# Newton's roots on VectorE for the gathered sums of a mixture-of-experts decoder, with two smaller moves

## The chip, the cores and the metric

The kernel runs on one core of a Trainium2 chip. A core has five engines with a queue of instructions each: TensorE (PE in the profile, with its weight loads as PEld), VectorE (DVE), ScalarE (ACT), GpSimd (POOL) and SyncE (SP), which issues most of the plain transfers. Indirect transfers, the gathers and scatters by an index, are issued by GpSimd. The metric is the device time of one execution in microseconds (us).

## The reference, cut to what matters

Four decoder layers work on 8 sequences of 256 tokens with 256 features. Each layer has a self-attention, a cross-attention and a feed-forward part; after each part the result is added to its input and normalised:

```python
def _layernorm(x, axis=-1, eps=1e-05):
    m = jnp.mean(x, axis=axis, keepdims=True)
    v = jnp.var(x, axis=axis, keepdims=True)
    return (x - m) / jnp.sqrt(v + eps)

x = _layernorm(x + _L0_attn_ref(x, ...))
x = _layernorm(x + _L0_xattn_ref(x, ctx_1024, ...))
x = _layernorm(x + _L0_ffn_ref(x, ...))
...                      # the same for L1, L2 and L3
```

The feed-forward parts of L0, L1 and L2 are mixtures of experts: a router scores the experts, every token takes its two best, and the two experts' outputs are added with weights. L1's has 8 experts with a limited capacity, so the place (rank) of a token in its expert's list matters:

```python
probs = jax.nn.softmax(xn @ router_w.T, axis=-1)
topk_p, topk_i = jax.lax.top_k(probs, K)          # K = 2
order = jnp.argsort(~sel, axis=1, stable=True)
dispatch = order[:, :capacity]
```

L3's first part is a state-space layer that begins with an RMS norm of x without a mean, `x * rsqrt(mean(x*x) + eps) * w`, and has no router anywhere.

## The kernel before

**Tiles.** The 2,048 tokens are 16 tiles of 128 tokens by 256 features (`NT`), two tiles to a sequence; a pair of tiles is a batch b (`NB` = 8), and four tiles are a block (`NBLK` = 4). The tiles of x stay on the chip from one part to the next. All of it is one program without loops at run time: Python generators write the instructions, and a scheduler decides the order of each engine's queue from the order in which they are written and from what depends on what. Pieces of one stage are put between those of another by hand: `self.later` appends a generator, and each `self.tick` takes one piece (up to the next `yield`) of the oldest one.

**Layer norm.** `norm` (L245) takes the mean and variance of a tile with `bn_stats` (L249) and `bn_aggr` (L251) on VectorE, then calls `rsqrt` (L179): two GpSimd instructions, the addition of eps (L182) and a power of −0.5 (L183). VectorE then subtracts the mean and multiplies by the root (L255). All layer norms of the kernel go through it.

**Routing.** `Routing.batch` (from L2484) routes one pair during the cross-attention, in pieces. The first piece is the scores, the softmax, the two best experts (`rhot`, `rsel` at L2535) and the running counts (`rbefore`, L2538). The next piece multiplies by a triangle and by ones on TensorE to count each token's rank (the helper `mm`, L155), works out the place in the expert's list (L2547 to L2560), and scatters the tile's rows there (L1018, GpSimd). In the kernel before, one empty piece stands between the two in L2 alone (`if kind == 2: yield`, L2540). In L0's and L1's cross-attention, `cross64`, the ticks stand in `outputs` between the products of the weights with V (L947), the transposes of the weights (L932) and the copies of these (L141 on VectorE, L143 on ScalarE).

**Gathered sums.** The next layer's attention takes the experts' outputs back: `Routing.collected().sums(b)` gathers two rows for each token of a pair (`gather`, L1055, into gy), adds them with their weights on VectorE (L2680), and calls `norm`. Two gy buffers for each of the two choices hold four gathers at most under way. In L0 to L1 and L1 to L2 the tiles are then transposed (`put_xT`, L235). An order is forced between one add and the next (`g.gate`).

**L3's first part.** From L2 to L3, `norm` also leaves the mean square of the normalised tile, v/(v+eps), in `ms` (L260). `block` (L1990) takes a root of four of these by `rsqrt` (`r4`), scales four tiles of x by it on GpSimd (`xb`, L1999) and transposes them on TensorE (L293) to `xr`. The products of the block follow (`steps`), and among them the step sizes dt by a chain of small VectorE instructions (L2014 to L2027) that ends in `ad`. In the first block, pieces of L3's keys (`l3_keys`, with a softmax whose last step is GpSimd's L2246) stand between. For each pair, `weights` makes decays (L2128 on ScalarE, L2130 on VectorE, exponentials L2140, products L2154), and `outputs` the gate (`zs`, L2180), the sum of squares on TensorE (`onec`) and the residual (L2196).

**Newton's roots.** `roots` (L1609) exists in the kernel before and is used for L2's and L3's wide statistics of 16 and 32 columns. It takes a first guess of 1/sqrt(v) from the bits of v by a shift and a subtraction, and improves it three times:

```python
        nc.vector.tensor_scalar(v, v, scale, eps, ALU.mult, ALU.add)
        nc.vector.tensor_single_scalar(u.bitcast(I32), v.bitcast(I32), 1, op=ALU.logical_shift_right)
        nc.vector.tensor_scalar(y.bitcast(I32), u.bitcast(I32), -1.0, float(0x5F3759DF), ALU.mult, ALU.add)
        for _ in range(3):
            nc.vector.tensor_tensor(u, y, y, ALU.mult)
            nc.vector.scalar_tensor_tensor(u, u, -0.5, v, ALU.mult, ALU.mult)
            nc.vector.scalar_tensor_tensor(y, u, 1.5, y, ALU.add, ALU.mult)
```

That is 12 VectorE instructions, each on the result of the one before. The buffer of u (`hu`) is single, that of y (`hy`) double.

Of the kernel before, what the change touches and what calls it, by code (L numbers as in the profile page):

```python
# [14 lines left out]
AF = mybir.ActivationFunctionType  # L15
ALU = mybir.AluOpType
# [4 lines left out]
P = 128  # L21
NB = 8
S = 256
D = 256
# [5 lines left out]
LN_EPS = 1e-5  # L30
# [31 lines left out]
class Build:  # L62
# [179 lines left out]
        self.norm(i, r)  # L242
        self.put_xT(i, self.X[i])

    def norm(self, i, r, square=False):  # L245

        nc = self.nc
        st = self.t(self.sm, [P, 6], "st")
        nc.vector.bn_stats(st, r)  # L249
        mv = self.t(self.sm, [P, 2], "mv")  # L250
        nc.vector.bn_aggr(mv, st)  # L251
        rs = self.t(self.sm, [P, 1], "rs")
        self.rsqrt(rs, mv[:, 1:2], 1.0, LN_EPS)
        t = self.t(self.xp, [P, D], "x", bufs=20)
        nc.vector.tensor_scalar(t, r, mv[:, 0:1], rs, ALU.subtract, ALU.mult)  # L255
        self.X[i] = t
        if square:
            if i % 4 == 0:
                self.ms[i // 4] = self.t(self.sm, [P, 4], "ms", bufs=2)
            nc.vector.scalar_tensor_tensor(  # L260
                self.ms[i // 4][:, i % 4 : i % 4 + 1], mv[:, 1:2], rs, rs, ALU.mult, ALU.mult
            )

    def add_row(self, i, row):

# [1340 lines left out]
        nc.vector.tensor_scalar(m, m, 1.0 / 16, None, ALU.mult)  # L1606
        nc.vector.tensor_tensor(v, v, m.unsqueeze(2).to_broadcast([rows, n, 16]), ALU.subtract)

    def roots(self, v, scale, eps):  # L1609

        nc = self.nc
        rows, n = v.shape
        y, u = (self.t(self.sm, [P, 32], name, bufs=k)[:rows, :n] for name, k in (("hy", 2), ("hu", 1)))
        nc.vector.tensor_scalar(v, v, scale, eps, ALU.mult, ALU.add)
        nc.vector.tensor_single_scalar(u.bitcast(I32), v.bitcast(I32), 1, op=ALU.logical_shift_right)  # L1615
        nc.vector.tensor_scalar(y.bitcast(I32), u.bitcast(I32), -1.0, float(0x5F3759DF), ALU.mult, ALU.add)
        for _ in range(3):
# [3 lines that stand above are left out]
        return y  # L1621
# [304 lines left out]
    def l3_attn(self):  # L1926
        nc, a = self.nc, self.a
        with ExitStack() as ctx:
# [61 lines left out]
            def block(blk):  # L1990

                self.need(2 * blk)
                out = xrs[blk] = self.t(w2, [P, 2, 512], "xr")
                r = self.t(self.sm, [P, 4], "r4")
                self.rsqrt(r, self.ms[blk], 1.0, 1e-5)
                yield
                for t in range(4):
                    x = self.t(self.tmp, [P, D], "xb")
                    nc.gpsimd.tensor_scalar(x, self.X[4 * blk + t], r[:, t : t + 1], 1.0, ALU.mult, ALU.mult)  # L1999
                    self.transpose_to(out[:, :, t * P : (t + 1) * P], x, 2)  # L2000
                yield
                yield from steps(blk, out)

            def steps(blk, xr):
# [36 lines left out]
                sts[blk] = dt, cs, csT.rearrange("p i s -> p (i s)")  # L2041

            front = block(0)
            for _ in range(2):
                next(front)
# [168 lines left out]
            for b in range(NB):  # L2214
                blk = b // 2
                if b % 2 == 0 and blk + 1 < NBLK:
                    following = block(blk + 1)
                    next(following)

                self.tick()  # L2220
                E, xd = weights(b, cv, *sts[blk])
                last = (b, cv, zs, E, xd)
                if b + 1 < NB:
                    if b % 2:
                        for _ in following:
                            pass
                    cv, zs = inputs(b + 1, xrs[(b + 1) // 2])
                    next(following, None)
                self.settle(1)
                self.later(outputs(*last))  # L2230
# [218 lines left out]
class Routing:  # L2449
# [34 lines left out]
    def batch(self, b):  # L2484
        g, nc, E, kind = self.g, self.g.nc, self.E, self.kind
        two = slice(2 * b, 2 * b + 2)
        f = lambda name, sh, dt=F32: g.t(g.keep, sh, name, dt, bufs=2)
        if kind:
            r = self.r[:, two]
# [5 lines left out]
        if kind == 2:  # L2495
            for t in range(2):
                x = g.t(g.keep, [P, D], "rx", bufs=2)
# [6 lines left out]
        m = f("rm", [P, 2])  # L2504
# [31 lines left out]
        for t in range(2):  # L2536
            i = 2 * b + t
            g.routed = nc.vector.tensor_tensor(self.before[:, i + 1, :], self.before[:, i, :], sel[:, t, :], ALU.add)  # L2538
        yield
        if kind == 2:  # L2540
            yield

        ps = g.ps()[:, : 2 * E].rearrange("p (t e) -> p t e", t=2)
# [126 lines left out]
    def collected(self):  # L2670


        g, nc = self.g, self.g.nc

        def sums(b):
            for i in (2 * b, 2 * b + 1):
                for k in range(2):
                    y = g.t(g.keep, [P, D], f"gy{k}", bufs=2)
                    g.gather(y, self.eo, self.src[:, k, i : i + 1])
                    add = nc.vector.scalar_tensor_tensor(g.X[i], y, self.wt[:, k, i : i + 1], g.X[i], ALU.mult, ALU.add)  # L2680
                    if g.gate is not None:
                        g.after(add.ins, [g.gate.ins])
                    if g.gates:
                        g.after(add.ins, [g.gates.pop().ins])
                    g.gate = add
                g.norm(i, g.X[i], self.kind == 2)

        sums(0)
        yield
        for b in range(NB):  # L2690
            if self.kind != 2:
                for i in (2 * b, 2 * b + 1):
                    g.put_xT(i, g.X[i])
            if b + 1 < NB:
                sums(b + 1)
            yield
# [194 lines left out]
```

## Time and profile before

The median of three runs is 3623.32 us (3618.66 to 3629.59). The profiled execution is another one: 3594.94 us, with a span of 3593.2 us and a mean granted TensorE clock of 0.896. All times inside the kernel are those of this execution, counted from the start of its span.

| stretch, us | what | TensorE busy | VectorE busy | ScalarE busy | GpSimd busy |
|---|---|---|---|---|---|
| 1069–1140 | L0's sums, start of L1's attention | 44.0 of 71 | 39.6 | 11.4 | 43.5 |
| 1140–1440 | rest of L1's attention | 278.6 of 300 | 165.9 | 89.9 | 34.0 |
| 1440–1712 | L1's cross-attention with routing | 246.9 of 272 | 188.1 | 85.9 | 74.6 |
| 2245–2318 | L1's sums, start of L2's attention | 59.4 of 73 | 39.6 | 19.0 | 42.6 |
| 2318–2560 | rest of L2's attention | 207.3 of 242 | 157.4 | 97.2 | 44.1 |
| 2994–3133 | L2's sums, L3's first block, keys | 100.8 of 139 | 75.3 | 30.4 | 71.1 |
| 3133–3370 | rest of L3's first part | 188.6 of 237 | 179.8 | 101.8 | 52.0 |

A line of the timeline gives start, duration, engine, source line, operation, output and inputs, shapes, and in brackets how long the engine stood idle before it and what released it. A line of the groups gives busy time, mean ns of one, and the idle time before. A wait is named "who waits <- for whom: us in total, times, longest".

### The profile page before, as it was taken

How to read it: one execution, taken by the hardware profiler on the slowest of the kernel's cores; microseconds unless marked ns; L12 is line 12 of the kernel's file. 1: busy time of each engine (PE TensorE's matmuls, PEld its weight loads, DVE VectorE, ACT ScalarE, POOL GpSimd, SP SyncE). 2: the span in 40 equal slices, each digit the busy share in tenths (PEclk: the TensorE clock that was granted, in tenths of full speed). 3: DMA queues.
4: the chain of work that ended last, by engine and by line, in shares of the span. 5: the costliest groups of instructions: out<-in, count | busy, mean ns of one | idle time of the engine just before them, and what ended most of it. 6: DMA issues, size and time to landing. Idle time of an engine off the chain costs nothing. (4 is left out here: it accounts for less than half of the span.)

```text
span 3593.2 us, 49384 instructions
## 1 busy us (share of the span) xinstructions
PE 3102.3 (86%) x19146; PEld 2184.7 (61%) x19146; DVE 1834.9 (51%) x4823; ACT 1043.6 (29%) x2343; POOL 928.1 (26%) x1398
## 2 busy tenths in 40 slices
PE   4777589979997998998999999898787997778789
PEld 3444257658875665666555777565555785566556
DVE  7888546631116555776211221566675344677652
ACT  4666322212222332332111111344222111343311
POOL 2222513243314101222000000411343444312351
PEclk6777689979998999988999999999777998888889
DMA  9900100035541000001010333200002552000000
GB/s 338 305 2 1 48 7 19 19 108 181 179 144 47 1 25 25 13 14 60 15 36 0 119 124 119 62 1 8 7 19 83 198 196 77 22 1 7 12 5 19
DMA packets 132127, 239.47 MB, mean 67 GB/s; under 512 B 14568, under 2 KB 103920, under 8 KB 124208
## 3 DMA queue, kind: packets, MB, share of 16 engines
q1 hardware_dynamic: 107632, 136.25, 11.3%
q0 software_dynamic: 23104, 98.95, 7.9%
q8 instruction: 154, 2.52, 0.3%
q10 hardware_dynamic: 1152, 1.05, 0.1%
q14 instruction: 85, 0.70, 0.1%
HBM read 156.52 MB, written 79.69 MB: 66 GB/s over the span
## 5 line engine op out<-in xcount | busy, mean ns | idle before, releaser
L155 PE MATMUL ps<-xt,w 128*128 128x256 f32 (+1 forms) x1408 | 452.9, 472 | 3.3 <-issue 2.9
L155 PE MATMUL ps<-w,hT 128*128 128x256 f32 (+1 forms) x1792 | 397.4, 379 | 0.0
L155 PEld LDWEIGHTS ps<-w,hT 128*128 128x128 f32 (+1 forms) x1792 | 329.9, 186 | 56.5 <-issue 6.0
L155 PE MATMUL ps<-gT,w 128*128 128x256 f32 (+1 forms) x1472 | 357.4, 401 | 5.7 <-ACT gT L143 3.0
L155 PEld LDWEIGHTS ps<-xt,w 128*128 128x128 f32 x1408 | 268.7, 198 | 149.4 <-issue 125.0
L155 PEld LDWEIGHTS ps<-gT,w 128*128 128x128 f32 x1472 | 276.5, 191 | 76.8 <-ACT gT L143 3.9
L155 PE MATMUL ps<-w,oT 128*128 128x256 f32 x768 | 181.9, 390 | 3.3 <-DVE mv L251 1.8
L267 POOL TENSOR_TENSOR xb<-x,rows 128x256 f32<-128x256 f32 x96 | 71.6, 752 | 401.7 <-DVE res L272 393.7
L155 PEld LDWEIGHTS ps<-w,oT 128*128 128x128 f32 x768 | 146.4, 194 | 38.5 <-issue 14.1
L235 PE MATMUL ps<-ident,x 128*128 128x128 f32 x320 | 62.0, 307 | 79.5 <-DVE x L255 59.4
L1115 ACT ACTIVATE hT<-ps,more 128x256 f32<-128x256 f32 x152 | 71.9, 474 | 196.1 <-PE ps L155 196.1
L255 DVE TENSOR_SCALAR x<-res,mv,rs 128x256 f32<-128x256 f32 x128 | 57.4, 449 | 126.9 <-POOL rs L183 126.9
L1126 DVE COPY y<-ps 128x512 f32<-128x512 f32 x41 | 28.3, 690 | 174.7 <-PE ps L155 174.7
L1184 DVE TENSOR_TENSOR hT<-hT,ps 128x512 f32<-128x512 f32 x56 | 38.5, 688 | 154.2 <-PE ps L155 152.7
L677 ACT ACTIVATE e<-ps,nm 128x128 bf16<-128x128 f32 (+1 forms) x256 | 103.9, 458 | 40.1 <-DVE nm L672 24.1
L932 PE MATMUL ps<-ident,P 128*77 128x128 f32 x512 | 90.0, 303 | 25.5 <-POOL P L923 15.7
L1666 POOL TENSOR_TENSOR kpad<-kpad,rows 128x256 f32<-128x256 f32 (+1 forms) x10 | 7.3, 729 | 404.2 <-DVE hu L1615 316.9
L923 POOL TENSOR_TENSOR P<-P,z 128x1232 f32<-128x1232 f32 x24 | 54.1, 2252 | 219.6 <-DVE z L921 214.3
L183 POOL TENSOR_TENSOR rs<-rs,mhalf 128x1 f32<-128x1 f32 x192 | 106.1, 554 | 14.2
L932 PEld LDWEIGHTS ps<-ident,P 128*77 128x77 f32 x512 | 60.7, 157 | 73.4 <-issue 25.5
L947 PE MATMUL ps<-PT,V 77*64 77x256 f32 x512 | 98.5, 446 | 7.5 <-DVE PT L141 4.9
L1180 ACT ACTIVATE hT<-ps 128x512 f32<-128x512 f32 x56 | 33.4, 597 | 237.5 <-PE ps L155 237.5
(655 smaller groups left out, 6319.2 us busy)
## 6 DMA issues: line engine op xcount, KB each, us to landing
l2x<-zero SPq DMA_DIRECT2D x28, 1024.0 KB, 11.3
l0x<-zero SPq DMA_DIRECT2D x16, 1024.0 KB, 11.3
w<-in_L_ffn_rg SPq DMA_DIRECT2D x8, 1024.0 KB, 7.0
w<-in_L_ffn_ru SPq DMA_DIRECT2D x8, 1024.0 KB, 5.0
w<-in_L_ffn_rd SPq DMA_DIRECT2D x8, 1024.0 KB, 5.7
l2e<-y SPq DMA_DIRECT2D x22, 256.0 KB, 2.3
rows<-in_rows SPq DMA_DIRECT2D x9, 544.0 KB, 3.7
l0e<-y SPq DMA_DIRECT2D x19, 256.0 KB, 2.9
```

The costliest lines, as they stand in the source:

```text
L155: self.nc.tensor.matmul(out, lhsT, rhs, start=(i == 0), stop=(i == last))
L183: self.nc.gpsimd.tensor_tensor(out, out, self.mhalf[: in_.shape[0], :w], ALU.pow)
L235: self.nc.tensor.transpose(ps[:, k * P : (k + 1) * P], x[:, k * P : (k + 1) * P], self.ident)
L255: nc.vector.tensor_scalar(t, r, mv[:, 0:1], rs, ALU.subtract, ALU.mult)
L267: self.nc.gpsimd.tensor_tensor(t, self.X[i], row, ALU.add)
L677: nc.scalar.activation(e[:, : (t + 1) * P], ps[j][:, i, :], AF.Exp, bias=nm[:, t, h : h + 1], accum_out=z[:, t, h : h + 1],)
L923: eng.tensor_tensor(pr, pr, z.unsqueeze(2).to_broadcast([P, H, SC]), ALU.mult)
L932: nc.tensor.transpose(psv[:, m, t * P : (t + 1) * P], Pt[t][:, 2 * n + m, :], self.ident)
L947: nc.tensor.matmul(po[64 * m : 64 * m + 64, :S], V[:, h * 64 : (h + 1) * 64], ahead[n % 2][:, m, :], start=True, stop=True,)
L1115: nc.scalar.activation(hT[:, f + m, :], ps[:, m * 256 : (m + 1) * 256], func, bias=more[:, f + m : f + m + 1])
L1180: nc.scalar.activation(hT[:, f, :], ps, func, **({"bias": bias(f)} if bias else {}))
L1184: nc.vector.tensor_tensor(hT[:, f, :], hT[:, f, :], ps, ALU.mult)
```

## The change

There are three edits.

- **Gathered sums.** `sums(b)` no longer calls `norm`. It takes the statistics of both tiles of the pair, then one `roots` on the two variances (128x2), then the two normalises. From L2 to L3, the mean squares of the pair come from two 128x2 multiplications. The layer norms outside the gathered sums keep `norm` and its GpSimd root. `norm` loses its argument `square`.
- **Rank products.** In `batch`, the empty piece between the counts and the rank products stands in L1 as well as in L2.
- **L3's scaled x.** `block` takes `r4` by `roots` on VectorE, and the four scalings of x are ScalarE activations (Copy with a scale per token). `roots` gets an argument `src`, so that it can read another tile than it writes.

```diff
-    def norm(self, i, r, square=False):
+    def norm(self, i, r):
...
-        if square:
-            if i % 4 == 0:
-                self.ms[i // 4] = self.t(self.sm, [P, 4], "ms", bufs=2)
-            nc.vector.scalar_tensor_tensor(
-                self.ms[i // 4][:, i % 4 : i % 4 + 1], mv[:, 1:2], rs, rs, ALU.mult, ALU.mult
-            )
...
-    def roots(self, v, scale, eps):
+    def roots(self, v, scale, eps, src=None):
...
-        nc.vector.tensor_scalar(v, v, scale, eps, ALU.mult, ALU.add)
+        nc.vector.tensor_scalar(v, v if src is None else src, scale, eps, ALU.mult, ALU.add)
...
-                r = self.t(self.sm, [P, 4], "r4")
-                self.rsqrt(r, self.ms[blk], 1.0, 1e-5)
+                r = self.roots(self.t(self.sm, [P, 4], "r4"), 1.0, 1e-5, self.ms[blk])
                 yield
                 for t in range(4):
                     x = self.t(self.tmp, [P, D], "xb")
-                    nc.gpsimd.tensor_scalar(x, self.X[4 * blk + t], r[:, t : t + 1], 1.0, ALU.mult, ALU.mult)
+                    nc.scalar.activation(x, self.X[4 * blk + t], AF.Copy, scale=r[:, t : t + 1])
...
         yield
-        if kind == 2:
+        if kind:
             yield
...
         def sums(b):
+            mv = g.t(g.sm, [P, 2, 2], "mv2", bufs=2)
             for i in (2 * b, 2 * b + 1):
...
-                g.norm(i, g.X[i], self.kind == 2)
+                st = g.t(g.sm, [P, 6], "st")
+                nc.vector.bn_stats(st, g.X[i])
+                nc.vector.bn_aggr(mv[:, i - 2 * b, :], st)
+            rs = g.roots(g.t(g.sm, [P, 2], "v2", bufs=2), 1.0, LN_EPS, mv[:, :, 1])
+            for i in (2 * b, 2 * b + 1):
+                t = g.t(g.xp, [P, D], "x", bufs=20)
+                k = i - 2 * b
+                nc.vector.tensor_scalar(t, g.X[i], mv[:, k, 0:1], rs[:, k : k + 1], ALU.subtract, ALU.mult)
+                g.X[i] = t
+            if self.kind == 2:
+
+                if b % 2 == 0:
+                    g.ms[b // 2] = g.t(g.sm, [P, 4], "ms", bufs=2)
+                m = g.ms[b // 2][:, 2 * (b % 2) : 2 * (b % 2) + 2]
+                nc.vector.tensor_tensor(m, rs, rs, ALU.mult)
+                nc.vector.tensor_tensor(m, m, mv[:, :, 1], ALU.mult)
```

## The prediction

> **What bounds the kernel now.** I read the busy shares first.
>
> ```profile
> PE 3102.3 (86%) x19146; PEld 2184.7 (61%) x19146; DVE 1834.9 (51%) x4823; ACT 1043.6 (29%) x2343; POOL 928.1 (26%) x1398
> ```
>
> TensorE is busy for 86% of the span. Only the other 491 us can be won, and only where the change touches what ends a TensorE wait. The view of waits names the ones concerned (total, times, longest):
>
> ```profile
> DVE x L255 <- POOL rs L183: 200.9, 176, 4.8
> POOL rs L182 <- DVE mv L251: 174.0, 100, 16.4
> PEld L155 <- DVE rsel L2535: 40.8, 17, 3.7
> ```
>
> The 200.9 us are VectorE's, mostly in layernorms that the change leaves alone. The groups by form split off the gathered sums: 48 normalises, with 58.8 us of idle time put down to the root.
>
> ```profile
> L255 DVE TENSOR_SCALAR x<-x,mv,rs 128x256 f32<-128x256 f32 x48 | 23.8, 496 | 59.5 <-POOL rs L183 58.8 <-POOL kv L2262 0.3
> ```
>
> Then the timeline, for what TensorE itself waits on. GpSimd between L0 and L1:
>
> ```profile
> 1112.80 0.96 POOL L1055 DMA_INDIRECT gy<-l0e,rsrc  x1 [0.30 <-issue]
> 1113.83 0.19 POOL L182 TENSOR_SCALAR rs<-mv 128x1 f32<-128x1 f32 x1
> 1114.29 0.97 POOL L1055 DMA_INDIRECT gy<-l0e,rsrc  x1 [0.27 <-issue]
> 1115.29 0.58 POOL L183 TENSOR_TENSOR rs<-rs,mhalf 128x1 f32<-128x1 f32 x1
> ```
>
> Roots and gather issues share one queue. A gather takes 1.25 us of it alone and the two root instructions of a tile about 1.0 us. The TensorE waits, one line from each place:
>
> ```profile
> 1135.34 0.59 PE L1278 MATMUL ps<-later,identb 128*128 128x512 bf16 x1 [11.91 <-DVE kT L1251]
> 2290.50 1.01 PE L1522 MATMUL ps<-ones,onesb 128*128 128x512 bf16 x2 [4.92 <-DVE w L1455]
> 3026.82 1.61 PE L293 MATMUL ps<-ident,xb 128*128 128x128 f32 x6 [5.11 <-POOL xb L1999]
> 3060.11 1.01 PE L155 MATMUL ps<-kv 77*128 77x128 f32 x4 [14.13 <-DVE w L2276]
> 1493.26 0.18 PE L155 MATMUL ps<-rsel,upper 128*128 128x8 bf16 x1 [1.15 <-DVE rsel L2535]
> 3300.47 0.81 PE L155 MATMUL ps<-ad,triu 128*128 128x8 f32 x3 [5.45 <-DVE ad L2027]
> ```
>
> **What the Trainium skill says.** "PSUM — Partial Sum Buffer", Engine vs sequencer instructions: the queues of ScalarE, VectorE and GpSimd are strictly first in, first out. The trace agrees: kT L1251 starts at 1134.60, just behind an add that waited for its gather until 1134.20. "VectorE: DVE Perf Modes", Rules for kernel authors: for chained operations the count matters; the trace has 0.17 to 0.19 us for each small L1614–L1620 instruction. "SBUF — State Buffer", two separate sides: VectorE and GpSimd lock a shared port pair against each other. Rarely seen here: one L1616 of 1.12 us against its usual 0.17. "ScalarE: Activation LUTs", What ACT_TABLE_LOAD costs: about 1.28 us and as much again of drain; the trace has the 1.28, and the next activation starts at once.
>
> **The change, part by part.** The instruction orders of the two programs, set side by side, give counts and places. GpSimd loses 120 instructions: 96 in 48 tile roots (48 × (0.19 + 0.55) = 36 us), 8 in four r4 roots (about 6 us) and 16 scalings (16 × 0.48 = 8 us), 50 us in all. VectorE gains 28 × 12 = 336 (at 0.17–0.19, about 60 us busy). ScalarE gains 16 scalings (nearest row: its 128x256 copy at 0.38, so 6 us) and two table loads (2.6 us). TensorE's and SyncE's counts stay. None of these totals is a time; that is worked out by place.
>
> *Roots alone.* Twelve dependent instructions took 0.21 us from start to start where they ran alone (2.5 us for a pair) and 0.10 where other work stood between. Before, a pair waited about 1 us per tile, more behind gathers.
>
> *L0 to L1.* The first pair's matmuls should start about 1 us sooner (two serial waits become one root). kT stands behind the add of the fifteenth gather after 1110.06. That was issued at 1131.34; fourteen pitches of 1.25–1.27 end at 1127.8. VectorE needs about 15 us of work in this stretch of some 20, roots included, so the gathers set the pace. The 11.91 us wait shrinks by 3.5. Together +4.5 us (0 to 6).
>
> *L1 to L2.* Gathers 4 to 27 were issued from 2257.51 to 2296.98, 1.72 us each; at 1.25–1.35 the last comes 8 to 10 us earlier. TensorE waits 2.71 + 2.87 + 4.92 + 3.14 = 13.6 us here, on L255 or on L1455 queued behind it. Four pairs' roots return up to 10 us to VectorE, which is half idle. I take half the waits, +6 (0 to 9).
>
> *L2 to L3.* Gathers run about 7 us earlier, but block 0's r4 is now twelve VectorE instructions that stand behind the roots of pairs 1 and 2 (hu has one buffer), and those wait for adds. I place r4 near 3033 (3026.2 before), so block 0's last transposes end 2.5 us later. The 14.13 us wait at 3060 is for a w copy queued behind an L255 and behind a GpSimd step at 3059.9, both late through roots and gathers: I put it at 3055, +5. Later key pieces wait 2.50 + 6.11 + 1.43 + 1.89 us at 3117–3132 on a GpSimd that now has less to do: +3. Together +8 (−6 to +12).
>
> *L3's blocks 1 to 3.* Scaled x now queues on ScalarE. Block 1: behind eight L2128, −1. Block 2: the fourth scaled x stands behind eight L2128 and an xr copy, near 3201 instead of 3197.6; two transposes and the onec products (3199.61) queue behind it, −2.3; VectorE's ad there moves ahead of an L2147, +0.7. Block 3: two extra loads and L2108 move L2128 and L2180 about 3.6 us later, so onec (3291.6) slips as much; but the dt chain that ends in ad no longer has two L2147 (0.69) and two L2154 (1.75) between its steps, so the 5.45 us wait nearly goes: +1.8. The xpad copies lose 0.3. Sum −1 (−7 to +3).
>
> *L1's rank products.* TensorE waits there 12.5 us in 8 pairs: seven times 1.15 to 1.4, and 2.97 in the last. Afterwards another L947 pair, four transposes and an L947 pair stand before them. Their PT is ready: one was copied by ScalarE long before, the other ends on VectorE (1456.81) ahead of rsel. rbefore and the rank instructions get behind a PT and an oT copy and their scatters come 2 us later, but the scatters are read only in the expert stage. The last pair's products go behind the shared expert's first half block, about 25 us later; l1x is loaded then, and TensorE first uses it at 2000.5. Cost covered; if it were not, SyncE's loads behind would slip by 25 us. +10 (0 to 12).
>
> *Other pairs of L1 and L2 attention.* TensorE is busy 279 of 300 us in L1's attention and 207 of 242 in L2's. A later pair's root runs under its matmuls, one pair ahead of need; where it shows, it costs some 0.2 us in each of 12 pairs: −2.5.
>
> Sum: 4.5 + 6 + 8 − 1 + 10 − 2.5 = 25 us. Made against the profiled execution, 3594.94 us: 3570. The median shown, 3623.32, stands 1.0079 above it, so 25.2 off the median: **3598 us**, 0.7% faster. Under 0.3%, 11 us, a measurement of this kernel can hardly tell a change from none.
>
> **Rivals.** *The wait only changes its name:* the adds still wait for landings (2.6 to 6.6 us from issue), VectorE's roots take what GpSimd gives back, and the rank wait comes again as a PT wait. For it: the adds at 1127–1138 wait 0.8 us each for their DMA, with no root near. Against: in 1110–1125 the pitch was 1.5, not 1.25. About 3 us stay: 3620. *ScalarE's queue eats half:* L3 at its bad end (−7), gathers half (9), ranks half (5), −2.5: about 5 us, 3618. *r4 decides, slower:* block 0's root is held on VectorE behind adds that wait for gathers. If r4 comes after about 3050 instead of 3033, the transposes (3034.4 before) end near 3055, the keys queue behind them, and 3060 becomes 3080. That is −20 there, the rest of L2 to L3 gives nothing, L3 loses 7, and the other parts give at most 14 of their 20: 13 us slower, 3636. Below 3040 it does not decide. For it: a single hu and an in-order queue; against: gathers 8 to 11 go out about 7 us earlier.
>
> **How the numbers follow.** Forecast 0.69, name only 0.09, ScalarE 0.08, r4 0.14. The first gives 0.69 faster plus a share of the middle two: faster 0.71, same 0.14, slower 0.15. All upper ends together (6 + 9 + 12 + 3 + 12 = 42) give 3581; I start the range at 3580 and end it at 3625, so that both middle rivals lie inside and r4 outside.
>
> **What would show it.** Instructions: GpSimd 1278, VectorE about 5160. The wait before the matmul at 1135 falls from 11.9 to about 8.4; the sum of TensorE waits for L1455 from 8 to about 4; no TensorE wait for rsel in L1, and no new wait of over 0.3 us before L947. r4 of block 0 at 3030–3036; the 14.13 wait ends 5 us sooner after the stage's start. onec in block 2 about 2 us later, and the wait for ad in block 3 under 2 us. Wrong would be: gathers still 1.45 us apart, roots over 3 us a pair, or r4 after 3040.

## The result and the profile after

The changed kernel takes 3617.16 us (median of 20 runs, 3609.66 to 3622.05) where the kernel before takes 3624.32 us beside it (20 runs, 3618.04 to 3629.59): a ratio of 0.9982 with a 95% interval of 0.9976 to 0.9988. The forecast was 3598 us, a ratio of 0.993. The sign was right, but of the 25 us only 7 came. That is less than the 0.3% taken as the limit of a measurement; with 20 runs on each side the interval still excludes no change.

One thing must be known to read this number. The runs of this case fell on chips of two kinds. On one kind the kernel before took 3595 to 3597 us as the median of a set of runs, on the other 3622 to 3625. The profiled execution that the forecast was worked out from (3594.94 us) is of the first kind, the three runs behind the median of 3623.32 are of the second, and so is the result. Below, "first kind" and "second kind" mean this, and a time is compared only with the kernel before in the same set. The five sets of experiments ran on five chips, so what in a chip, or around it, makes the kind is not told apart.

The profile after is of the second kind: its execution took 3614.42 us, its span is 3612.7. First the busy shares of the changed kernel:

```profile
PE 3119.9 (86%) x19135; PEld 2195.5 (61%) x19146; DVE 1880.5 (52%) x5159; ACT 1053.4 (29%) x2361; POOL 871.9 (24%) x1278
```

The instruction counts are those of the forecast: 120 fewer on GpSimd, 336 more on VectorE, 18 more on ScalarE (16 scalings and two table loads). Next its view of waits (total, times, longest), the lines that answer to those shown of before, and two that are new:

```profile
DVE x L254 <- POOL rs L183: 138.5, 141, 2.9
...
PEld L155 <- DVE rsel L2527: 25.5, 10, 3.2
...
PE ps L155 <- issue: 24.0, 17, 9.6
...
PE ps L286 <- ACT xb L1991: 19.5, 4, 12.1
```

VectorE's waits for GpSimd's root fell by 62 us, and seven of the 17 waits for rsel are gone, out of L1's eight. The last two lines had no part in the forecast: TensorE stands 24.0 us with nothing to wait for ("issue" is time without a releaser that the profile shows), and four times it waits for a scaled x that ScalarE now writes. In the groups by form, the normalises of gathered sums wait for no root any more, 0.8 us instead of 59.5:

```profile
L2686 DVE TENSOR_SCALAR x<-x,mv,hy 128x256 f32<-128x256 f32 x48 | 19.8, 453 | 0.8 <-DVE x L2673 0.2
```

And its timeline at the places of the forecast (start, duration, then the idle time before and what ended it):

```profile
1136.37 0.95 POOL L1048 DMA_INDIRECT gy<-l0e,rsrc  x1 [0.30 <-DVE hy L1613]
1137.62 0.95 POOL L1048 DMA_INDIRECT gy<-l0e,rsrc  x1 [0.30 <-issue]
...
1131.94 0.58 PE L155 MATMUL ps<-xt,w 128*128 128x256 f32 x1 [1.55 <-issue]
...
2290.45 0.58 PE L1515 MATMUL ps<-ones,onesb 128*128 128x512 bf16 x1 [1.28 <-DVE w L1448]
...
3068.08 1.02 PE L155 MATMUL ps<-kv 77*128 77x128 f32 x4 [5.78 <-DVE v L1607]
...
1466.37 0.18 PE L155 MATMUL ps<-rsel,upper 128*128 128x8 bf16 x1
```

Gathers now follow one another at 1.25 us. The wait of 11.91 us for kT is no longer there, but not because kT is earlier: TensorE gets there late, since its xt,w products trickle out one per 1.4 to 2.1 us without a wait. The 4.92 us for w at 2290 are 1.28, the 14.13 us for w at 3060 are 5.78, the wait before the rank products is gone, and so is the one for ad in block 3.

To find where the time went, the same matmul was matched in two TensorE queues, and the change of its distance to its counterpart was taken over each stage, in us (minus is time saved). The first kind is from a run told below, the second is the result's profile against one of the kernel before on that kind.

| stage | forecast | first kind | second kind |
|---|---|---|---|
| L0 to L1 | −4.5 | −3.0 | +3.7 |
| L1's cross-attention (rank products) | −10 | −28.5 | −17.1 |
| L1 to L2 | −6 | −5.5 | +0.4 |
| later pairs, up to L2's cross-attention | +2.5 | +6.1 | +6.8 |
| L2 to L3 | −8 | −10.5 | −10.3 |
| L3's blocks 1 to 3 | +1 | +15.2 | +12.1 |
| rest | 0 | −1.5 | −2.6 |
| sum | −25 | −27.7 | −7.0 |

### The profile page after: what moved, and what is told of

Its sections match the earlier page's. It is cut to its first block, busy times and chain, and to the rows that moved or that the text cites. A ratio compares the mean times of both kernels' runs of the same rounds, so it can differ in the third digit from the quotient of the medians.

```text
span 3612.7 us, 49584 instructions
## 1 busy us (share of the span) xinstructions
PE 3119.9 (86%) x19135; PEld 2195.5 (61%) x19146; DVE 1880.5 (52%) x5159; ACT 1053.4 (29%) x2361; POOL 871.9 (24%) x1278
## 5 line engine op out<-in xcount | busy, mean ns | idle before, releaser
L235 PEld LDWEIGHTS ps<-ident,x 128*128 128x128 f32 x320 | 41.7, 161 | 102.4 <-issue 48.4
L1525 DVE SCALAR_TENSOR_TENSOR f<-ps,f 128x512 f32<-128x512 f32 x128 | 79.3, 682 | 33.8 <-ACT f L1524 33.8
```

Source lines behind the costliest of these rows:

```text
L235: self.nc.tensor.transpose(ps[:, k * P : (k + 1) * P], x[:, k * P : (k + 1) * P], self.ident)
L1525: nc.vector.scalar_tensor_tensor(f[:, j], ps[j], 1.0, f[:, j], ALU.max, ALU.min)
```

## The experiments

Theory A, from the forecast: each part gives what its sum says. Rivals after the result: one part costs what another gives (L3 above all); or the parts are worth what was said on the chip that the profile came from, and the second kind differs.

**Each part alone, and two of them together (first kind).** "sums" takes only the changes in `sums`, `norm` and `roots`; "ranks" only the first diff below; "block" only the second.

```diff
-        if kind == 2:
+        if kind:
             yield
```

```diff
-                r = self.t(self.sm, [P, 4], "r4")
-                self.rsqrt(r, self.ms[blk], 1.0, 1e-5)
+                r = self.roots(self.t(self.sm, [P, 4], "r4"), 1.0, 1e-5, self.ms[blk])
...
-                    nc.gpsimd.tensor_scalar(x, self.X[4 * blk + t], r[:, t : t + 1], 1.0, ALU.mult, ALU.mult)
+                    nc.scalar.activation(x, self.X[4 * blk + t], AF.Copy, scale=r[:, t : t + 1])
```

> The gathered sums alone get Newton's roots on VectorE; ranks and L3's block are as before. Theory 1 (the profile after): the sums win only between L2 and L3, where the matmul stream gained 11 us, and nothing between L0 and L1 (2 to 3 us lost there) and between L1 and L2 (0.5 us lost): 5 to 10 us faster than before. Rival (the prediction): all three places win, 15 to 18 us faster. Second rival: VectorE's 288 small instructions return what GpSimd gives: within 4 us of before.

> L1's rank products one piece later, nothing else. Theory 1 (the profile after shows 14 us won in L1's cross-attention, 4 us of them given back where the shared expert begins): 9 to 14 us faster than before, and no TensorE wait for rsel in L1. Rival: what was won there is the noise of two executions, and the wait comes back for a PT copy: under 4 us.

> L3's block alone: r4 by Newton's steps on VectorE and scaled x by ScalarE; the sums and ranks are as before. Theory 1 (the matmul stream lost 16 us between 3126 and 3412 in the profile after, in steps behind the scaled x of ScalarE and behind gates that ScalarE takes later): 9 to 16 us slower than before. Rival (the prediction, block 1 to 3 at -1): within 4 us of before.

> The sums and the ranks together, L3's block as before. Theory 1: the sum of the two alone, 14 to 24 us faster than before and 8 to 16 us faster than the changed kernel. Rival: L3's block has no cost of its own, and this is within 4 us of the changed kernel, 7 us faster than before.

Against 3596.96 us of before: sums 3576.14 (ratio 0.9946, interval 0.9933 to 0.9959), ranks 3576.66 (0.9941, 0.9928 to 0.9954), block 3608.11 (1.0033, 1.002 to 1.0046), sums and ranks together 3544.14 (0.9853, 0.984 to 0.9866). Two parts give 20 us each and together more than their sum; the third costs 11. Ranks, and the two together, gave more than was expected of them (9 to 14 and 14 to 24 us). Of the 12 us that the two together give beyond their sum, 8 lie in L1's cross-attention, where this trace gained 28.4 us and that of ranks alone 20.5. The part that the forecast put at about nothing is the one that loses.

The sums do what the forecast's chain said. The timeline of "sums" at the end of L0 to L1:

```profile
1133.77 0.59 PE L1271 MATMUL ps<-later,identb 128*128 128x512 bf16 x1 [8.50 <-DVE kT L1244]
```

The wait for kT fell from 11.91 to 8.50 us; 8.4 was forecast. But the first pair is not 1 us sooner, as one root for two serial waits had suggested: the pair's single root now stands behind the adds of both its tiles, and the wait in front of the transposes is 14.56 us in one piece where it was 10.03 and 2.54.

**The whole change and the two parts beside each other (second kind).**

> The changed kernel itself, beside the kernel without its L3 part. Theory (the clock): the three parts have the effects seen alone, -21, -20 and +11 us, and the sums and the ranks together -53; so this is 35 to 45 us faster than before on a chip where before takes 3597. Rival: the L3 part costs more in company than alone, because r4 now waits behind the roots of the sums on VectorE: 5 to 25 us faster than before. Where it falls on the kind of chip that took 3624 us for before, the ratio is the first one again, 0.998.

> The sums and ranks without the L3 part again, on the same chip as the changed kernel. On the chip of the first runs: 0.985 again. On the other kind of chip: if the L3 part is what took the gain, 0.985 to 0.990 there too; if the chip is (its matmul stream showed issue gaps of 10 us twice that no other trace has), 0.995 to 1.000.

> The sums, the ranks and r4 on VectorE; the scaled x stay on GpSimd. If the L3 loss is ScalarE's queue and what the scheduler makes of it: within 4 us of the sums and ranks. If it is r4's place on VectorE behind other roots: within 4 us of the changed kernel.

> The sums, the ranks and the scaled x on ScalarE; r4 stays on GpSimd. If the L3 loss is ScalarE's queue: within 4 us of the changed kernel, 10 us or more slower than the sums and ranks. If it is r4: within 4 us of the sums and ranks.

Beside 3624.83 us: the whole change 3613.55 (0.9972, 0.9964 to 0.998), without the L3 part 3596.89 (0.993, 0.9917 to 0.9943). "Root only" adds r4 by Newton's steps to sums and ranks and leaves the scaling on GpSimd: 3602.22 (0.9935, 0.9922 to 0.9948). "Scale only" adds the scaling on ScalarE and leaves r4 on GpSimd: 3611.59 (0.9967, 0.9954 to 0.998). So the L3 part costs 17 us here, and ScalarE's scaling most of it: it alone costs 15, the root alone 5 in the medians (the intervals overlap, so a cost of the root is not shown).

**The first kind again, with the kernel before as a control for the profile.**

> The kernel before, unchanged, for its trace. If this is the kind of chip where it takes about 3624 us: where the 28 us over the first profiled execution (3595) lie. If the issue gaps at the gathers are the chip's, it shows them too (10 us each in the starts of L1's attention and L2's experts); if they need the changed order, it does not. On the other kind of chip: 3593 us again.

> The changed kernel. On the chip of the first experiments, if the L3 part costs there what it cost against the sums and ranks elsewhere (17 us): 3558 to 3564 us against 3597, ratio 0.990. If it costs only what it cost alone (11 us): 3553 to 3557. On the other kind of chip: 0.997 again.

> L1's rank products one piece later, alone. On the chip of the first experiments: 0.994 again. On the other kind, if a half-clock stretch after each rank wait is what doubles the gain and the clock falls there for other reasons anyway: 8 to 12 us faster only; if not, 18 to 22 us.

> The gathered sums alone. On the chip of the first experiments: 0.9946 again. On the other kind, if the issue gaps fill the wait for kT that the faster gathers shorten: 15 us faster or less, the L0 to L1 stage without gain; if not, 19 to 23 us.

The kernel before gives 3594.44 us in one run, and its trace lies within 0.5 us of the first one in every stage. So differences between traces of this kind are mostly the kernels'; one stage is less steady, that of the rank products, where three traces of ranks gain 20.5, 23.0 and 28.4 us. The whole change takes 3567.19 (0.9915, 0.99 to 0.9931), 2.8 us under the 3570 that the forecast's sum gave for this kind, and above the 3553 to 3564 expected after the runs before. Ranks 3574.13 (0.9939), sums 3574.1 (0.9941), as before.

The pair "sums and ranks" and "whole change", both of the first kind, shows what the L3 part does: 21 us over the stages from 2990 on. First r4. Where GpSimd has it ("sums and ranks"):

```profile
2991.52 0.19 POOL L182 TENSOR_SCALAR r<-ms 128x4 f32<-128x4 f32 x1 [0.21 <-DVE hy L1609]
...
2992.95 2.08 POOL L1992 TENSOR_SCALAR xb<-x,r 128x256 f32<-128x256 f32 x4
```

Where VectorE has it (the whole change):

```profile
2992.62 0.17 DVE L1607 TENSOR_SCALAR r<-ms 128x4 f32<-128x4 f32 x1
2992.70 0.16 DVE L1611 TENSOR_TENSOR hu<-hy 128x2 f32<-128x2 f32 x1
...
2996.37 0.16 DVE L1608 TENSOR_SCALAR hu<-r 128x4 int32<-128x4 int32 x1
...
2999.21 1.31 ACT L1991 ACTIVATE xb<-x,hy 128x256 f32<-128x256 f32 x3 [4.00 <-DVE hy L1613]
```

The root of the first block begins at 2992.62, and its second instruction comes 3.75 us later: between them stands the root of the third pair (the L1611 on hu of two columns), which holds the one buffer of hu. The scaled x starts at 2999.21 instead of 2992.95; 1.1 us of that the two traces were apart already. This is the mechanism of the rival "r4 decides", at a price of 5 to 6 us and not of 20.

Then the scaled x of the later blocks. "Sums and ranks", TensorE and ScalarE:

```profile
3147.45 0.44 PE L286 MATMUL ps<-ident,xb 128*128 128x128 f32 x2 [0.42 <-POOL xb L1992]
3213.25 0.44 PE L286 MATMUL ps<-ident,xb 128*128 128x128 f32 x2 [0.82 <-POOL xb L1992]
...
3275.46 0.63 ACT L2173 ACTIVATE zs<-w 128x512 f32<-128x512 f32 x1 [1.78 <-POOL w L2169]
...
3277.23 2.58 ACT L2121 ACTIVATE l2s<-ps,cs 128x256 f32<-128x256 f32 x8
```

The whole change:

```profile
3160.82 0.44 PE L286 MATMUL ps<-ident,xb 128*128 128x128 f32 x2 [3.78 <-ACT xb L1991]
3228.48 0.44 PE L286 MATMUL ps<-ident,xb 128*128 128x128 f32 x2 [2.90 <-ACT xb L1991]
...
3289.53 2.58 ACT L2120 ACTIVATE l2s<-ps,cs 128x256 f32<-128x256 f32 x8
3291.95 1.19 ACT L2172 ACTIVATE zs<-w 128x512 f32<-128x512 f32 x2
```

In blocks 2 and 3 the fourth scaled x of a block comes 3.4 and 2.1 us later than on GpSimd (3.78 − 0.42, 2.90 − 0.82), with the onec products right behind. Another 1.9 us go by up to block 3's onec, where two more table loads and a large exponential stand in ScalarE's queue. The wait for ad in block 3 (5.45 us) goes, as forecast, and gives 3.8 to 4.8 us back. Then the order of ScalarE's queue turns: the two zs stand behind the eight l2s instead of ahead of them, and onec, which reads them, slips by 5 us. These shifts at single places add to some 8 of the 15 us of blocks 1 to 3 (3.4 + 2.1 + 1.9 − 4.8 + 5 = 7.6).

The stage as a whole shows what they amount to. In the view of windows, the first number after the length of the stretch is TensorE's busy time, with its matmuls in brackets, and the third from the right is the clock granted to TensorE, 1 being full speed. Blocks 1 to 3 in "sums and ranks", then in the whole change:

```profile
3082.10:3361.50 279.40, 219.63 (x1249) 178.97 (x1249) 200.88 (x501) 107.51 (x173) 65.66 (x106) 0.85 0.02 7
...
3090.30:3385.10 294.80, 236.41 (x1248) 192.98 (x1249) 206.19 (x535) 115.51 (x187) 61.36 (x96) 0.80 0.02 6
```

The stage is 15.4 us longer, but TensorE is not idle longer: 59.8 us (279.40 − 219.63) became 58.4. New waits for the scaled x are paid for by waits that went, ad's above all. The loss is busy time: the same matmuls take 16.8 us more, at a clock of 0.80 instead of 0.85, which is about 118 us of the stage at half clock instead of 84 (0.20 × 294.8 × 2 and 0.15 × 279.4 × 2). "Block" alone shows the same beside the kernel before: 59.7 us idle against 59.9, 231.3 busy against 219.1. So does the second kind: 279.1 us without the L3 part and 289.7 with it, 59.6 and 58.6 of them idle. So what the L3 part costs in these blocks is TensorE's clock. Which of its delays lowers the clock was not tried. The clock of this stage also moves by itself: two traces of ranks, which change nothing here, are 3 and 6 us longer in it than the kernel before, again with the same idle time.

**The kernel before and two parts on the second kind.**

> The kernel before, unchanged, for its trace; sent again because the last call fell on the kind of chip where it takes 3595 us. On the other kind (3624 us): if the two stretches in which TensorE's own issue is slow (10 us each, at the starts of L1's attention and of L2's experts) are that chip's with any order, they show here too; if they need the changed order, TensorE's issue gaps sum to 5 us or less here and the 28 us lie elsewhere.

> The rank products alone. On the chip that takes 3624 us for before: 18 to 22 us faster if the parts keep their worth and only the sums lose there; under 12 us if the half-clock stretches that it removes elsewhere come back for other reasons.

> The gathered sums alone. On the chip that takes 3624 us for before: under 10 us faster if it is their gain that the slow issue of TensorE in the gather stretch eats; about 20 us if it is not.

The kernel before takes 3621.47 us in one run (3622.03 as the median of 9), ranks 3606.21 (0.9956, 0.994 to 0.9973), sums 3611.99 (0.9969, 0.9956 to 0.9982). So the sums are worth 10 us here and 21 on the first kind; that is where the two kinds part most. The trace of the kernel before, alike in every instruction, is 26.5 us longer on this kind. The longer places are L0's cross-attention (6.9 us), L1's (3.1), the start of L2's experts (11.6) and L3 (3.3). Its view of waits has lines that no trace of the first kind has:

```profile
ACT hT L1119 <- issue: 27.6, 7, 5.1
...
DVE y L1126 <- issue: 18.7, 6, 7.4
...
PE ps L1073 <- issue: 17.1, 1, 17.1
```

Engines stand for microseconds with nothing to wait for. On the first kind such lines exist for weight loads and GpSimd, and for TensorE only as one or two single waits (2.87 and 1.36 us in the kernel before, 1.36 in the changed one and in "sums"). On the second kind they come with any program, changed or not, and where they fall depends on it: with the sums changed, at 1124 to 1144, in the very stretch where kT was to be 3.4 us sooner (the lines shown of after), so L0 to L1 gives nothing. In L1 to L2 the waits for w shrink as on the first kind (1.28 us is left in after), but the first pair comes 2.8 us later and 2.2 us of such standing appear. What makes the issue slow was not tried: these records don't show it.

**Why the ranks give twice their waits.** The waits for rsel in L1 add to 12.5 us; the stage gained 17 to 28. The view of windows for the kernel before over the stage of the rank products and over 13.6 us behind one of its waits, then for ranks (the last run below) over the same work as in the first line:

```profile
1440.00:1712.00 272.00, 246.90 (x1421) 175.70 (x1420) 188.13 (x576) 85.88 (x193) 74.58 (x102) 0.87 0.09 29
...
1494.80:1508.40 13.60, 13.60 (x85) 11.13 (x86) 10.22 (x28) 5.02 (x11) 4.26 (x4) 0.50 0.11 39
...
1435.90:1679.50 243.60, 221.54 (x1418) 157.12 (x1417) 184.19 (x555) 85.43 (x193) 71.97 (x102) 0.98 0.10 33
```

Of the 28.4 us between the first line and the last, only 3.0 are idle time of TensorE (272.00 − 246.90 = 25.1, and 22.1 with ranks). The waits for rsel fell from 12.5 to 1.9 us, but those for P (L923, VectorE) grew from 6.1 to 12.4 and those for PT from 2.6 to 4.0. The other 25 us are busy time: the same matmuls run at a clock of 0.98 instead of 0.87. On the second kind the idle time does not fall at all (23 us before, 26 with ranks), and the stage still gains 17.

1.5 us after the wait that ends at 1493.26, the clock is at a half for 13.6 us. There are six such stretches, 72 us in all (0.13 × 272 × 2 = 71); four of them begin 1.1 to 2.6 us after one of the waits for rsel. With ranks or the whole change it is 14 to 41 us on the same stage, with sums or block alone still 72. This may be the waits for rsel, or the new order of the work. Two kernels were made to tell it apart. Both keep the old order and put eight matmuls into each pair that nobody reads, the first ahead of the rank products, where TensorE waits, the second behind them; the third is ranks once more. All three ran on one chip of the first kind.

```diff
+        full = g.ps()
+        ps = full[:, : 2 * E].rearrange("p (t e) -> p t e", t=2)
+        if kind == 1:
+            for _ in range(8):
+                nc.tensor.matmul(full[:, P : 2 * P], g.ident, g.ident, start=True, stop=True)
         for t in range(2):
             g.mm(ps[:, t, :], [(g.upper, sel[:, t, :]), (g.onesb, self.before[:, 2 * b + t, :])])
```

> The kernel before, with its waits for rsel in L1's pairs left as they are, but eight matmuls of 128x128 whose result nobody reads stand just ahead of each pair's rank products and fill the wait (about 8 x 0.13 = 1 us of work in 1.15 us of wait). No wait is taken away. If it is TensorE's idle time in these pairs that costs it its clock, the stretches of half clock between 1440 and 1712 fall from six to two or fewer and the kernel is 5 to 11 us faster than before (0.997 to 0.9985), although the products start no sooner. If the half clock has another cause (the order of the matmuls, GpSimd's and the DMAs' work beside it), nothing changes: 1440 to 1712 as long as before, or some 0 to 3 us longer where the filling sticks out.

> The control: the same eight matmuls a pair, put behind the rank products, so that the wait stays idle. If idle time is the cause: the half-clock stretches stay (four or more in L1's attention) and the 64 added matmuls cost their own time, 8 to 12 us in this stretch (1.0015 to 1.0035). If the added work itself lifts the clock: as fast as the kernel whose wait is filled.

> The rank products a piece on alone, on the same chip as the two others, for scale: 0.994 to 0.9956, as on two chips earlier. If idle time is the cause, it lies below the kernel with the filled wait by about the 8 to 12 us of wait that it takes away.

Against 3596.08 us: filled wait 3576.14 (0.9945, 0.9932 to 0.9959), the same matmuls behind the wait 3601.78 (1.0015, 1.0008 to 1.0021), ranks 3576.16 (0.9946, 0.9933 to 0.996). The filled wait in the timeline and the windows:

```profile
1493.36 1.95 PE L2547 MATMUL ps<-ident 128*128 128x128 f32 x16
1495.14 0.17 PE L155 MATMUL ps<-rsel,upper 128*128 128x8 bf16 x1
...
1552.55 0.99 PE L932 MATMUL ps<-ident,P 128*77 128x128 f32 x7 [1.50 <-DVE P L923]
...
1660.34 1.56 PE L932 MATMUL ps<-ident,P 128*77 128x128 f32 x6 [3.50 <-DVE P L923]
...
1440.00:1712.00 272.00, 250.75 (x1597) 179.84 (x1597) 193.89 (x594) 90.18 (x200) 75.75 (x106) 0.97 0.11 34
```

The filling takes 1.78 us a pair, more than the wait of 1.15, so the rank products come later in their pair than before, and still the stage is 19.7 us shorter: the clock is 0.97 there instead of 0.87. As much as moving the rank products gives (20 us in the medians) comes from keeping TensorE busy in front of them, in the old order. The size that was expected, 5 to 11 us, was too small by half. The control fits less neatly. It costs 5.7 us, as the idle-time theory had it, but the clock of the same window rose to 0.94 too, with three half-clock stretches instead of the four or more expected, and 20 us of added work (1.96 us a pair at full clock, 3.3 to 3.7 in three pairs at half) made the stage only 7.4 us longer. Over the same work of the kernel before, in us:

| kernel | stage | TensorE busy | of it unread | idle | waits for rsel | clock |
|---|---|---|---|---|---|---|
| before | 272.0 | 246.9 | 0 | 25.1 | 12.5 | 0.87 |
| filled wait | 253.0 | 231.8 | 16 | 21.2 | 0 | 0.97 |
| behind the wait | 279.3 | 245.5 | 20 | 33.8 | 12.5 | 0.93 |
| ranks | 243.6 | 221.5 | 0 | 22.1 | 1.9 | 0.98 |

So the unread work speeds up the rest in both places, by 31 us inside the wait (246.9 − 231.8 + 16) and by 22 behind it (246.9 − 245.5 + 20), where every wait for rsel is still there. Nor does the length of a wait decide alone: the waits for P are longer (1.4 to 1.5 us, line 1552.55), stand in most pairs of the filled kernel, and no half-clock stretch comes until 1660.37. That one begins at a wait of 3.50 us (line 1660.34). So the clock seems to follow how busy TensorE is around a wait; over which window, and which work counts, these runs don't say.

## Why the prediction was right or wrong, step by step

**TensorE's clock** is the step that failed all through: the forecast summed TensorE's waits and put what its clock does at nothing, without a reason. In the two stages that missed most, on the first kind, TensorE's idle time changed by −3.0 us (ranks) and −1.4 us (L3's blocks), and the stages by −28 and +15. The two terms below that are wrong by 18 and 14 us are wrong by this.

**The sum against the profiled execution** held, by luck: 3570 was worked out, 3567.19 measured on a chip of that kind, because two errors cancel: ranks 18 us too small a gain, L3's blocks 14 us too small a loss.

**The step from the profiled execution to the median** failed too. The forecast took 3594.94 to 3623.32 as one kernel's scatter and carried the gain over by the factor 1.0079. The two numbers are of two kinds of chips, and the gain is not the same on them: 27.7 us in the trace on one, 7 to 11 on the other. The terms that shrank are L0 to L1 (−4.5 forecast, +3.7), L1 to L2 (−6, +0.4) and, against the first kind, the ranks. By the table, the 18 us that the result lacks are these two gather stages (14.6), L3's blocks (11.1) and the later pairs (4.3), less what the ranks, L2 to L3 and the rest gave beyond their forecast (12.0). All three runs of before lay at least 0.6% above its profiled execution (3618.66 to 3594.94), where the runs among themselves agreed within 0.3%; that was the sign.

**L0 to L1, L1 to L2** (first kind): the pitch of the gathers, the kT wait (8.50 for 8.4) and the waits for w were right, and −3.0 and −5.5 came for −4.5 and −6. The term of the first pair was wrong in sign: the pair's root waits for the adds of both tiles, 1.7 us later and not 1 us sooner. Of the four waits of L1 to L2 that were read as waits for L255 and L1455, the trace gives no releaser for the one of 2.87 us.

**L2 to L3** came out in size: −10.5 and −10.3 for −8, on both kinds. The place of r4 was right (its scaled x starts at 2999.21 in a stage that begins 32.4 us earlier, so at 3031.6 in the time of the kernel before, where r4 was put near 3033), and so was the reason (one hu, VectorE in order). But two errors cancel here as well: without the L3 part the stage gains 17.5 us on the first kind, twice the forecast, almost all of it idle time (41.0 us before, 25.2 in "sums"), and the L3 part takes 7 of that back.

**L3's blocks 1 to 3**: a loss of 1 us was forecast and 12 to 15 were lost, where the bad end of the range was a loss of 7. The waits were near: the fourth scaled x 2.3 late (3.4 and 2.1 measured), onec of block 3 3.6 (about 4), ad's wait gone; and the sum of TensorE's idle time hardly moved. It did not look at what follows ad in block 3, where the zs of the last group went behind eight l2s in ScalarE's queue and onec came 5 us later. The term that is missing is the clock, 0.80 for 0.85, and 16.8 us of busy time with it. The rival "ScalarE's queue eats half" named the place and ended at 3618, 1 us from the result, by luck: its composition (L3 −7, gathers half, ranks half) is not what the traces show.

**The rank products** won for another reason than was argued: 10 forecast, 17 to 28 measured. The forecast had the wait itself gained, since nothing behind it would take it back. The traces show that the waits for P and PT took back 8 of the 11 us, and that nearly all of the gain is the clock. The Trainium skill, "TensorE: Matmul & The Clock Gate", Part 1, says that TensorE falls to half its clock after an idle window of about 3.4 us. The stretches in these traces are indeed near multiples of 3.4 us (13.65, 10.24 and 6.83), and the wait of 3.50 us in the filled kernel is followed at once by 6.8 us at half clock. But in the kernel before, the longest wait of the stage is 3.3 us, the stage is 91% busy (246.90 of 272), and 72 us of it are at half clock, so a gap as long as the page's window is not needed; the measurement decides. Nearer to this case is the page's section "A second HAM failure mode", where a kernel's short idles between groups of matmuls let its clock go up and down; the filled wait agrees with it, the waits for P that leave the clock alone do not. The forecast read PE's busy share and never the clock of the stage.

**The other pairs** cost 6 to 7 us and not 2.5. On the first kind sums alone shows 2.4 and 5.8 us in two runs, so it comes with the sums. But TensorE's idle time there is 77.6 and 76.5 us in these runs and 76.9 before: the roots don't show as waits, and the cost is busy time again.

**The rival "name only"** was right about the rank waits, which came back as waits for P and PT, and wrong about what follows from it. Its other half is out on both kinds: the gathers keep their 1.25 us.

## What to carry to other kernels

Before carrying a gain from a profile to a median, look whether the runs lie about the profiled execution at all; a gap that every run shows can be another kind of chip, and a gain made of short waits need not survive there. On the engine that bounds the kernel, read busy time, idle time and granted clock of a whole stage over the same work: here a wait that was removed mostly came back under another name, and what was won or lost was the clock. Where a wait cannot be removed, work that nobody reads may win as much, and its place matters. Moving small work to an idle engine is judged by what stands behind it in that engine's queue to the end of the stage, and by the clock of the engine that waits for it. Here the best version leaves the L3 part out: sums and ranks alone take 0.9853 of the time before on the first kind and 0.993 on the second, better than both kernels.

## What the runs showed of the hardware that was not expected

Chips differ: one program took 3595 to 3597 us in three sets of runs and 3622 to 3625 in three, and on the slower kind ScalarE, VectorE and TensorE have waits without a releaser of 63.0, 18.7 and 17.1 us, where the faster kind has none of ScalarE and VectorE and 4.2 us of TensorE. TensorE's clock was at a half for 72 us of a 272 us stage that was 91% busy, in stretches of mostly 13.6 us, and eight unread matmuls in each wait for rsel took that to 14. A stage can grow by 15 us with the idle time of the engine that bounds it unchanged (59.8 and 58.4 us).
